# The last step of a recurrent scan in two halves of positions, with the end rows reordered in time

## The chip, the cores and the metric

One core of one Trainium2 chip runs the whole kernel. The metric is device time in microseconds (us). TensorE is PE in the profile (its weight loads PEld), VectorE is DVE, ScalarE is ACT, GpSimd is POOL, and SyncE (SP) issues all the DMAs of this kernel.

## The reference

The input is r of 8 x 2048 x 512 (batch, position, channel). A first part adds to it the normalized result of a long convolution with a state-space kernel; it is unchanged here. Call its result x. The second part is a gated recurrence over the batch axis, 8 steps, for each of the 2048 positions:

```python
def step(c, xt):
    ft = jax.nn.sigmoid(xt @ wf.T + c @ uf.T + bf)
    it = jax.nn.sigmoid(xt @ wi.T + c @ ui.T + bi)
    gt = jnp.tanh(xt @ wc.T + c @ uc.T + bc)
    c = ft * c + it * gt
    return (c, None)
c_final, _ = lax.scan(step, c0, x)
h = jnp.tanh(jnp.einsum('tbi,oi->tbo', x, wo) + c_final @ uo.T + bo)
...
x = x + _layernorm(h)
```

Here xt is the layer norm of x at step t. The output h at every step needs c_final of its position, the state after the last step: for any position, nothing of the output can be finished before all 8 steps are done.

## The kernel before

**Tiling.** The 2048 positions are cut into 4 blocks of 512 (`q`), each of four chunks of 128 (`cj`). Blocks follow one another; in each, 8 steps (`t`) follow one another, so there are 32 (block, step) pairs, about 64 us each. A matrix product of 512 x 512 by 512 x 512 is done by a scheme of seven products of 256 x 256 blocks (`FIRST` holds four of them, `THEN` three), each in split half precision with three products, so a gate *unit* is 42 matmuls with x and 42 with the state. A unit makes one gate (`kind` 0 forget, 1 input, 2 candidate) for one of two halves of the gate's rows (`mp`); there are six units in a step, and two *z units* (42 matmuls each) which make x @ wo.T and store it in `z_d`. Each moving operand is 256 columns (`BP`), the positions.

A unit's PSUM tile `u` (name `u`, pool `pu`, three buffers) holds four 256-wide sums. `part_a` (L974) does the matmuls of `FIRST` and then, on ACT (L993) and DVE (L994 to L997), the sums between them; `part_b` (L999) does those of `THEN` and the gate's tanh on ACT (L1021). With kind 2 DVE joins two gates (L1026), with kind 0 it makes the new state (`state`, L1030: L1041, L1042). After a block's last step the state is split into two half-precision tiles `cf` (ACT L1047, DVE L1051).

**Order of the work.** The order on PE, ACT, DVE, POOL and SP is the program's own. `put` hangs functions on numbered places, 16 to a step, and `go(p)` calls those of place p after a unit's part has been issued; so an instruction stands in its engine's queue behind all that was issued before it, and a DMA that waits holds up the DMAs behind it on SP. In a step, part a of one unit is followed by part b of the unit before. Into the steps of block q are woven `turn` (the next step's x, transposed and split), `prep` (the next rows of x) and the *heads* of block q-1 (`head`, L1130): for each of its 32 rows of 128 positions x 512 channels they load z, add the product of the final state on POOL (L1136), take tanh on ACT (L1139), norm statistics on DVE, the scale on POOL, the normalization on ACT (L1153) and the last sum on POOL (L1154), and store. A head starts every 3 places.

**The end.** The last block has no later block to hide in. After its last step, `last` (L1072) makes the four chunks' output sums (c_final @ uo.T), 48 matmuls of 512 columns into two `u` tiles; the 512 x 512 weights `uw` and the bias `bo` were loaded during the step. All four chunks need the state of all positions to be done. `out` (L1102) adds the bias in place (DVE L1104). Then 16 *rows* (`tail`, L1161), each of two steps of one chunk, go through these stages, `n` being the row:

```python
        for n in range(len(rows) + 5):
            if n % 4 == 0 and n < len(rows):
                end[10 + n // 4]()
            for st_, d in ((0, -3), (1, -3), (6, 5), (2, 1), (3, 2), (4, 3), (5, 3)):
                if 0 <= n - d < len(rows) and (st_ > 1 or n - d > (2 if st_ else 8)):
                    rows[n - d][st_]()
```

Stages 0 and 1 load z and x, stage 2 adds the output sum to z on DVE (L1187, one input in PSUM) and takes tanh on ACT (L1188), stage 3 is the norm's statistics on DVE (L462, L464, L465) and the scale on POOL (L471, L475, L476), stage 4 the normalization on ACT (L1195), stage 5 the last sum (L1200, on POOL; of every fourth row one half on DVE), stage 6 the store (L1203). The z and x of the rows lie in tiles that the weights and gates have left.

Of the kernel before, what the change touches and what calls it, by code (L numbers as in the profile page):

```python
# [22 lines left out]
NB = 8  # L23
# [36 lines left out]
def s4_gated_block(ctx, tc, a, dbg=None):  # L60
# [897 lines left out]

    def views(key):
        q, t, kind, n = key  # L960
        xf = xfs[q, t]
        if kind == "z":
# [4 lines left out]
        return ((lambda f, b, l, k: w[:, k, f, int(l), ms], lambda f, b, l, k: xf[:, b, int(l), k]),  # L967
                (lambda f, b, l, k: uw[:, k, f, int(l), ms], lambda f, b, l, k: cf[k][:, b, int(l)]))
# [5 lines left out]
    def part_a(key):  # L974

        q, t, kind, n = key
        z = kind == "z"
        u = units[key] = pu.tile([P, 4, BP], F32, name="u")
        for pr in FIRST:
            mms(u, places(key, pr), *views(key)[0], True, not t or z)  # L980
        if t and not z:
            mms(u, FIRST[0][:1] + FIRST[1] + FIRST[0][1:], *views(key)[1], False, True)
# [4 lines left out]
        else:  # L987
            g = gates[key] = FJ.tile([P, 4, BP], F32, name="gate2", tag="wq") if kind == 2 else FT.tile([P, 4, BP], F32, name=f"gate{kind}")
            c22 = g[:, 2]
        z_, v_ = (UV, UZ) if z else (UZ, UV)  # L990
        u2 = u2p[:, len(u2s) % 2]
# [5 lines left out]
        V.tensor_tensor(u[:, 2:4], u[:, 2:4], u2[:, None].to_broadcast([P, 2, BP]), ALU.add)  # L997

    def part_b(key):  # L999

        q, t, kind, n = key
# [23 lines left out]
        if kind == 2:  # L1025
            V.scalar_tensor_tensor(g, gates.pop((q, t, 1, n)), 1.0, g, ALU.add, ALU.mult)  # L1026
        elif kind == 0:
            return state(q, t, n)

    def state(q, t, n):  # L1030

        f, ig = gates.pop((q, t, 0, n)), gates.pop((q, t, 2, n))
        if t == 0:
            cds[q, n] = FT.tile([P, 4, BP], F32, name=f"cd{n}")
        cd = cds[q, n]
        for h in range(2):
# [6 lines left out]
            if t == NB - 1:  # L1043
                if h == 0:
                    cf = FT.tile([P, 4, 2, BP], F16, name=f"cf{n}", bufs=2 - n)
                    cfs.setdefault((q, t), []).append(cf)
                S.activation(cf[:, hs, 0], cd[:, hs], AF.Copy)  # L1047
# [24 lines left out]
    def last(q):  # L1072
# [3 lines left out]
        def load():  # L1076
            if end:
                u4 = FE.tile([P, KT, 2, H], F16, name="uw", tag="xf")
# [9 lines left out]
        def load_b():  # L1088
            bo = FE.tile([P, H], F32, name="bo", tag="xa", bufs=2) if end else FT.tile([P, H], F32, name="bo", tag="x1r", bufs=2)
            dma(out=bo, in_=a["bo"])  # L1090
            uws.append(bo)

        def sums(cj, ks=(0, 1, 2, 3)):
            cf, i, cs = cfs[q, NB - 1], cj // 2, slice(cj % 2 * P, (cj % 2 + 1) * P)
            if cj not in us:
                us[cj] = us[cj - 1] if end and cj % 2 else pu.tile([P, 4, BP], F32, name="u").rearrange("p (a b) c -> p a (b c)", a=2)
            for k in ks:
                b = ((0, 3), (1, 2))[i][k // 2]
                mm3(us[cj][:, cj % 2], lambda l: cf[k % 2][:, b, l, cs], lambda l: uws[k][:, l], start=(k == 0), stop=(k == 3))

        def out(cj):
            p_ = us[cj][:, cj % 2]  # L1102
            if end:
                V.scalar_tensor_tensor(p_, uws[KT], SW, p_, ALU.mult, ALU.add)  # L1104
                us_[QC * q + cj] = p_
# [14 lines left out]
        if end:  # L1120
            return [load, load_b] + [lambda ks=ks, cj=cj: sums(cj, ks) for ks in ((0, 2), (1, 3)) for cj in range(QC)] + each[1::2]
# [39 lines left out]
    def tail(q, cj, tp, n):  # L1161

        c, s_ = QC * q + cj, {}

        def load():
            w = (3, 1, 5, 2, 6, 0)[n // 3]
            if n % 3 == 0:
                tails[w] = (FW if w < 2 else FV if w == 2 else FT).tile([P, 3, 2, H], F32, name="zz", tag=f"w{w}", bufs=1)
            s_["z"] = tails[w][:, n % 3]
            dma(out=s_["z"], in_=z_d[c, :, 2 * tp : 2 * tp + 2])  # L1170

        def load_x():
            i = (n + 3) % 9
            if n == 15:
                s_["x"] = tails[0][:, 1]
            elif i < 3:
                if i == 0:
                    tails[4] = FT.tile([P, 3, 2, H], F32, name="xw", tag="w4", bufs=1)
# [187 lines left out]
```

## Time and profile before

| What | us |
|---|---|
| median of three runs (2801.1 to 2802.04) | 2801.32 |
| the profiled execution | 2797.84 |
| its span, first to last instruction | 2796.0 |
| PE busy in the span | 2538.4 (91%) |
| DVE, ACT, POOL busy in the span | 2076.8, 1474.4, 1224.0 |
| first matmul of the last step | 2650.64 |
| first of the 48 output sums on PE | 2718.76 |
| DVE's first bias sum (L1104) | 2726.73 |
| issue of the last store | 2792.49 |

The page gives each engine's busy time, then 40 equal slices of the span with the busy share in tenths, then the chain of work that ended last, followed back from the last instruction. In a timeline each line is a start, a length, the engine, the line of code, the operation with its output and inputs, and how many were merged. In a table by windows each engine has its busy time and number of instructions, then come the granted PE clock, the share of the DMA engines and GB/s. Matmuls are pipelined: the distance between two starts is their price, not the length of one.

### The profile page before, as it was taken

To read this page: it belongs to the slowest core of one execution; us is meant where nothing else is said; L and a number is where in the kernel's file an instruction comes from. 1 tells how busy PE (TensorE), PEld (TensorE's weight loads), DVE (VectorE), ACT (ScalarE), POOL (GpSimd) and SP (SyncE) were. 2 spreads that over 40 slices of the span, in tenths; PEclk is the share of its full clock that TensorE was granted. 3 is DMA by queue.
4 is the path that set the end of the run, shared out by engine and by line. 5 is a ranking of instruction groups with operands and counts; after the bars stand their busy time and mean duration, and the time that the engine had idled before them with its cause. 6 is when DMAs were issued, how large, how long until landed. Compare 5 with 4: busy or idle time off the path is not lost.

```text
span 2796.0 us, 59846 instructions
## 1 busy us (share of the span) xinstructions
PE 2538.4 (91%) x23892; PEld 2225.9 (80%) x23892; DVE 2076.8 (74%) x4208; ACT 1474.4 (53%) x3075; POOL 1224.0 (44%) x1520
## 2 busy tenths in 40 slices
PE   4578888896999999999999999999999999999990
PEld 3367777785888888888888887888888788888880
DVE  8878888867667766577887777778777577776748
ACT  8966666654444444445555544455555445544436
POOL 5767777743112211114554531355544124543317
PEclk9799999998999999999999999999999999999995
DMA  6977887887335433235665532355554335543247
GB/s 237 311 232 243 256 257 245 260 282 208 106 75 132 113 90 85 95 91 142 162 178 150 144 103 91 108 165 170 155 165 134 95 94 154 165 124 102 91 168 250
DMA packets 507535, 449.24 MB, mean 161 GB/s; under 512 B 275574, under 2 KB 386680, under 8 KB 502264
## 3 DMA queue, kind: packets, MB, share of 16 engines
q1 hardware_dynamic: 506824, 444.90, 52.9%
q8 instruction: 186, 3.05, 0.4%
q14 instruction: 93, 0.76, 0.1%
q10 hardware_dynamic: 432, 0.52, 0.1%
HBM read 293.58 MB, written 151.78 MB: 159 GB/s over the span
## 4 chain that ended last, share of the span: by engine, by line
PE 63%; DVE 6%; ACT 3%; issue 1%; POOL 1%; DMA 1%; SPq 0%; POOLq 0%; DVEq 0%; ACTq 0%
PE u L955 61%; PE pt L485 2%; DVE u L997 1%; DVE zz L1187 1%; ACT gate L1021 1%; ACT xf L101 0%; PE u L450 0%; DVE sth L462 0%; DVE u2p L994 0%; DVE xf L102 0%; PE u L452 0%; PE u L451 0%; DVE cd L1042 0%; ACT zr L1153 0%; ACT cf L1064 0%
## 5 line engine op out<-in xcount | busy, mean ns | idle before, releaser
L955 PEld LDWEIGHTS <-w 128*128 128x128 f16 x15120 | 1480.8, 98 | 203.2 <-issue 18.9
L955 PE MATMUL u<-xf,w 128*128 128x256 f16 x8064 | 944.1, 273 | 22.9 <-ACT gate L1021 9.6
L955 PE MATMUL u<-cf,w 128*128 128x256 f16 x7056 | 825.6, 273 | 1.2 <-DVE cf L1066 1.2
L1021 ACT ACTIVATE gate<-u,bias 128x512 f32<-128x512 f32 (+1 forms) x384 | 201.0, 574 | 282.4 <-PE u L955 282.1
L993 ACT ACTIVATE u2p<-u 128x256 f32<-128x256 f32 x256 | 96.6, 379 | 425.2 <-PE u L955 425.0
L955 PE MATMUL u<-w,xf 128*128 128x256 f16 x2688 | 310.8, 273 | 3.7 <-DVE u L997 3.7
L1154 POOL TENSOR_TENSOR x1r<-x1r,zr 128x512 f32<-128x512 f32 x96 | 133.5, 1391 | 407.4 <-ACT zr L1153 298.8
L994 DVE TENSOR_TENSOR u2p<-u2p,u 128x256 f32<-128x256 f32 x256 | 106.7, 417 | 275.2 <-ACT u2p L993 273.7
L909 POOL TENSOR_TENSOR xr<-y,xr 128x512 f32<-128x512 f32 x120 | 160.6, 1358 | 304.0 <-ACT y L908 304.0
L955 PEld LDWEIGHTS <-xf 128*128 128x128 f16 x2688 | 263.2, 98 | 36.1 <-DVE u L997 5.2
L997 DVE TENSOR_TENSOR u<-u,u2p 128x512 f32<-128x512 f32 x256 | 179.0, 699 | 8.8
L646 POOL TENSOR_TENSOR u<-xg,u 128x512 f16<-128x512 f32 x104 | 129.1, 1241 | 107.6 <-ACT u L644 106.6
L471 POOL TENSOR_TENSOR rsy<-rsy,nhalf 128x2 f32<-128x2 f32 (+1 forms) x68 | 50.2, 739 | 283.2 <-DVE rsy L465 282.0
L640 POOL TENSOR_TENSOR xg<-xg,mu 128x512 f32<-128x512 f32 x112 | 162.3, 1455 | 6.7 <-DMA xg<-in_xr 6.7
L102 DVE TENSOR_TENSOR x<-pxt,x 128x256 f16<-128x256 f32 x240 | 100.0, 418 | 63.6 <-ACT x L101 62.2
L1026 DVE SCALAR_TENSOR_TENSOR gate<-gate,gate 128x1024 f32<-128x1024 f32 x64 | 90.0, 1406 | 69.5 <-ACT gate L1021 68.3
L1136 POOL TENSOR_TENSOR zr<-zr,ur 128x512 f32<-128x512 f32 x96 | 131.2, 1367 | 21.1 <-DMA zr<-z_d 12.7
L462 DVE BATCH_NORM_STATS2 sty<-y 128x6 f32<-128x512 f32 x120 | 76.9, 681 | 77.1 <-DMA y<-y_d 77.1
L666 PE MATMUL pxt<-x,at 128*128 128x256 f16 x224 | 61.8, 276 | 79.4 <-DVE x L102 78.8
L101 ACT ACTIVATE x<-pxt 128x256 f16<-128x256 f32 x240 | 91.5, 382 | 74.4 <-PE pxt L666 68.7
L451 PE MATMUL pyt<-u,t 128*128 128x128 f16 (+2 forms) x544 | 124.0, 228 | 0.0
L452 PE MATMUL pyt<-u,t 128*128 128x128 f16 (+2 forms) x544 | 123.5, 227 | 0.0
(375 smaller groups left out, 5204.8 us busy)
## 6 DMA issues: line engine op xcount, KB each, us to landing
xs<-in_rr SPq DMA_DIRECT2D x32, 1024.0 KB, 6.0
t<-kpad SPq DMA_DIRECT2D x32, 1024.0 KB, 5.6
y_d<-y SPq DMA_DIRECT2D x30, 1024.0 KB, 7.6
xr<-in_r SPq DMA_DIRECT2D x60, 512.0 KB, 5.5
xa<-x_d SPq DMA_DIRECT2D x120, 256.0 KB, 4.0
y<-y_d SPq DMA_DIRECT2D x59, 512.0 KB, 5.9
x_d<-xr SPq DMA_DIRECT2D x59, 512.0 KB, 3.2
xg<-in_xr SPq DMA_DIRECT2D x28, 1024.0 KB, 8.2
```

Source lines behind the costliest of these rows:

```text
L102: V.tensor_tensor(lo, src, hi, ALU.subtract)
L451: T.matmul(out, lhsT=w(1), rhs=x(0), start=False, stop=False)
L452: T.matmul(out, lhsT=w(0), rhs=x(1), start=False, stop=stop)
L640: Q.tensor_tensor(xg, xg, bc(mu1), ALU.subtract)
L646: (V if g == 2 else Q).tensor_tensor(u[:, js, 1], xg, u[:, js, 0], ALU.subtract)
L909: Q.tensor_tensor(xv, yv, xv, ALU.add)
L955: T.matmul(u[:, d], lhsT=w(f, b, i == 1, k), rhs=x(f, b, i == 2, k), start=opens and bank not in seen, stop=stop and j == len(n) - 1, skip ...
L994: V.tensor_tensor(u2, u2, u[:, UY], ALU.add)
L997: V.tensor_tensor(u[:, 2:4], u[:, 2:4], u2[:, None].to_broadcast([P, 2, BP]), ALU.add)
L1021: act = lambda o, s_, b: S.activation(o, s_, AF.Tanh, scale=gsc[kind], bias=b)
L1136: Q.tensor_tensor(s_["z"], s_["z"], us_[c], ALU.add)
L1154: Q.tensor_tensor(s_["x"], s_["x"], s_["z"], ALU.add)
```

## The change

Three things, all in the last block.

1. In the last step each gate unit is made twice, for positions 0 to 127 and 128 to 255 of the 256 columns (`half`); all six units of the first half, `g`, come before the six of the second, `h`. The z units stay whole. In the 512 positions of the block the first half is chunks 0 and 2, the second chunks 1 and 3. The output sums of chunks 0 and 2 are issued between units of the second half.
2. The end's rows are numbered by chunk in the order 0, 2, 1, 3, and every stage of a row gets a place of its own, written as a time in us from the step's start (`US` turns it into places). Rows 0 to 5 add the output sum on POOL, from a bias sum kept in SBUF; rows 6 to 15 on DVE. One scale on POOL serves two rows (four norms) and now does the addition of epsilon too.
3. The heads of the block before start every 2.5 places instead of every 3, and the tiles that hold z, x, `uw` and `bo` are others.

The core of the diff (loads, tiles and index plumbing left out):

```diff
+    def half(key):
+
+        return slice(key[4] * P, (key[4] + 1) * P) if len(key) > 4 else slice(0, BP)
...
-        u = units[key] = pu.tile([P, 4, BP], F32, name="u")
+        open_(key)
+        fill(key)
+
+    def open_(key):
+
+        t, z = key[1], key[2] == "z"
+        u = units[key] = pu.tile([P, 4, BP], F32, name="u")[:, :, 0 : P if len(key) > 4 else BP]
         for pr in FIRST:
             mms(u, places(key, pr), *views(key)[0], True, not t or z)
+
+    def fill(key):
+
+        q, t, kind, n = key[:4]
+        z, u = kind == "z", units[key]
+        w = u.shape[-1]
         if t and not z:
             mms(u, FIRST[0][:1] + FIRST[1] + FIRST[0][1:], *views(key)[1], False, True)
...
-                V.scalar_tensor_tensor(p_, uws[KT], SW, p_, ALU.mult, ALU.add)
-                us_[QC * q + cj] = p_
+                o = p_ if cj % 2 else FE.tile([P, H], F32, name="ue", tag="xa", bufs=2)
+                V.scalar_tensor_tensor(o, uws[KT], SW, p_, ALU.mult, ALU.add)
+                us_[QC * q + cj] = o
...
+        cj, tp = (0, 2, 1, 3)[r // 4], r % 4
...
+            pair("z", z_d, "rows" if r in (6, 7) else ((7, 3, None, 1, 5, 2)[(r + (r > 7)) // 3], (r + (r > 7)) % 3))
...
+            pair("x", x1_d, ("wl", "y", "ws", "rows", (4, 1), (4, 2), "wl", "y", (2, 2), (6, 0), (6, 1), (6, 2), (0, 0), (0, 1), (0, 2), (4, 0))[r])
 
         def sum_():
+            for z in s_["z"]:
+                (Q if r < 6 else V).tensor_tensor(z, z, us_[c], ALU.add)
+
+        def gate():
+            for z in s_["z"]:
+                S.activation(z, z, AF.Tanh, scale=1.0 / SW)
+
+        def stat():
+            if m == 0:
+                both[0] = [FE.tile([P, 2, *d], F32, name=nm, bufs=2) for nm, d in (("mvb", (2, 2)), ("rsb", (2,)), ("nmb", (2,)))]
+            mv, rs, nm = s_["b"] = both[0]
+            st = FE.tile([P, 2, 6], F32, name="stb", bufs=2)
             for i in range(2):
-                z = s_["z"][:, i]
-                V.tensor_tensor(z, z, us_[c], ALU.add)
-                S.activation(z, z, AF.Tanh, scale=1.0 / SW)
-
-        def stat():
-            s_["s"] = lnscale(lnstat([s_["z"][:, i] for i in range(2)], "h"))
+                V.bn_stats(st[:, i], s_["z"][i])
+            for i in range(2):
+                V.bn_aggr(mv[:, m, i], st[:, i])
+
+        def scale():
+            mv, rs, nm = s_["b"]
+            Q.tensor_scalar(rs, mv[:, :, :, 1], EPS, None, ALU.add)
+            Q.tensor_tensor(rs, rs, nhalf[:, 0:4].rearrange("p (a b) -> p a b", a=2), ALU.pow)
+            Q.tensor_tensor(nm, mv[:, :, :, 0], rs, ALU.mult)
+            Q.tensor_scalar(nm, nm, -1.0, None, ALU.mult)
...
+            for i, (z, x) in enumerate(zip(s_["z"], s_["x"])):
+                (V if i and (r > 13 or r % 4 == 3) else Q).tensor_tensor(x, x, z, ALU.add)
...
     def go(p):
-        for f in todo.pop(p, ()):
-            f()
+        for k in sorted(k for k in todo if k <= p):
+            for f in todo.pop(k):
+                f()
...
-                p = 3 * r + 17 - 16 * t
+                p = (3 * r if q < NQB - 1 else (5 * r + 1) // 2) + 17 - 16 * t
...
+    put((load_uo, load_bo), PL, (2, 4))
+    for p, cj in ((21, 0), (25, 2)):
+        put((lambda cj=cj: end_sums(cj), lambda cj=cj: end_out(cj)), PL, (p, p + 1))
+    for ks, p in (((0, 2), 31), ((1, 3), 31.5)):
+        put([lambda ks=ks, cj=cj: end_sums(cj, ks) for cj in (1, 3)], PL, (p, p))
+    US = 1 / 2.6
+    put([lambda cj=cj: end_out(cj) for cj in (1, 3)], PL, (88 * US, 88.5 * US))
+    for r, p in enumerate((3, 3, 3, 11, 11, 11, 20, 20, 28, 28, 28, 28, 28, 28, 30, 30)):
+        put(rows[r][:1], PL, (p,))
+    for r, p in enumerate((12, 12, 12, 20, 31, 31, 85 * US, 88 * US, 30, 30, 30, 30, 31.2, 31.2, 31.2, 31.2)):
+        put(rows[r][1:2], PL, (p,))
+    began = (60, 62.6, 65.2, 67.8, 70.4, 73, 82.5, 85.5)
+    scaled = (75.6, 77.4, 86.6)
+    outs = (79, 81.6, 84, 88, 94, 96.5)
+    for r, f in enumerate(rows):
+        t0 = began[r] if r < 8 else 89 + 3 * (r - 8)
+        t1 = t0 + (5.5 if r < 6 else 1.4)
+        t2 = scaled[r // 2] if r < 6 else 92 + 6 * (r // 2 - 3)
+        t3 = (77.5, 79, 81, 82.5)[r] if r < 4 else t2 + 2 + 1.5 * (r % 2)
+        t4 = outs[r] if r < 6 else t2 + 6.4 + 2.5 * (r % 2)
+        put(f[2:5], PL, (t0 * US, t1 * US, (t1 + (2.5 if r < 6 else 1.5)) * US))
+        if r % 2:
+            put(f[5:6], PL, (t2 * US,))
+        put(f[6:], PL, (t3 * US, t4 * US, (t4 + 2.6) * US))
...
+        q, t = steps[NL]
+        zs = [(q, t, "z", i) for i in range(2)]
+        g, h = [[(q, t, gt, mp, i) for mp in range(2) for gt in (1, 2, 0)] for i in range(2)]
+        A, B = lambda k: [(part_a, k)], lambda k: [(finish, k)]
+        O, F = lambda k: [(open_, k)], lambda k: [(fill, k)]
+        plan = (A(zs[0]) + B(before) + A(zs[1]) + B(zs[0]) + O(g[0]) + O(g[1]) + F(g[0]) + F(g[1]) + B(zs[1]) + B(g[0])
+                + sum((A(k) + B(k_) for k, k_ in zip(g[2:] + h, (g + h)[1:])), []) + B(h[5]))
+        for p, (f, key) in enumerate(plan):
+            f(key, PL + p) if f is finish else f(key)
+            go(PL + p)
+        go(PL + 1000)
```

Place p of the last step is `PL + p`; the list `plan` has one entry per place 0 to 30, A(k) being part a of unit k and B(k) part b, and the places are called in the order of their numbers. The stages' times only order the instructions of each engine; no instruction waits for a time.

## The prediction

> **What bounds the kernel now.** I read first the page's 40 slices (PE full until the last slice, where its clock falls to 5 tenths), then the chain of work that ended last from 2640 us on, then the table by windows, then the timeline of the end. The windows cut the last step and what follows it:
>
> ```profile
> core 0: us, PE busy (x) PEld busy (x) DVE busy (x) ACT busy (x) POOL busy (x), PEclk, DMA share, GB/s
> 2650.00:2719.00 69.00, 69.00 (x634) 61.75 (x632) 34.83 (x63) 23.57 (x49) 10.11 (x14) 1.00 0.46 155
> 2719.00:2730.00 11.00, 10.28 (x48) 4.48 (x46) 7.21 (x12) 4.09 (x8) 0.00 (x0) 1.00 0.68 258
> 2730.00:2750.00 20.00, 0.00 (x0) 0.00 (x0) 19.54 (x44) 13.79 (x22) 15.15 (x23) 0.58 0.48 154
> 2750.00:2770.00 20.00, 0.00 (x0) 0.00 (x0) 19.50 (x41) 14.30 (x22) 18.00 (x28) 0.50 0.81 276
> 2770.00:2796.00 26.00, 0.00 (x0) 0.00 (x0) 16.70 (x33) 12.48 (x19) 20.74 (x27) 0.50 0.75 283
> ```
>
> Until 2719 PE has no gap and DVE, ACT and POOL are half idle or more. Then PE does 48 output sums and stops, and the 16 end rows run alone on DVE (97% busy) and POOL. The chain agrees: PE to 2726.5, then DVE's row instructions, POOL's last sums, the last store at 2792.5, end at 2796.0. So the step is PE's, the 66 us behind it are DVE's and POOL's, and the two stages hardly overlap. One end row reads so:
>
> ```profile
> 2768.18 1.27 DVE L1187 TENSOR_TENSOR zz<-zz,u 128x512 f32<-128x512 f32 x2
> ...
> 2769.38 1.27 DVE L462 BATCH_NORM_STATS2 sth<-zz 128x6 f32<-128x512 f32 x2
> ...
> 2769.61 2.48 POOL L1200 TENSOR_TENSOR xx<-xx,zz 128x512 f32<-128x512 f32 x2
> ...
> 2770.58 0.29 DVE L464 BATCH_NORM_AGGREGATE mvh<-sth 128x2 f32<-128x6 f32 x2
> 2770.98 1.14 DVE L465 TENSOR_SCALAR rsh<-mvh 128x2 f32<-128x2 f32 x1
> ...
> 2772.03 1.27 DVE L1187 TENSOR_TENSOR zz<-zz,u 128x512 f32<-128x512 f32 x2
> ```
>
> Start to start, DVE needs 1.20 (sum) + 1.20 (statistics) + 0.40 (aggregate) = 2.8 us a row; the rest of the 3.85 is L465, two numbers per partition, 0.17 us when POOL is free and 1.14 here, ending just as POOL's L1200 ends (2772.09). Over the end the 16 L465 took 11.3 us. The same blocking shows in DVE instructions with both inputs in SBUF and never in those with one input in PSUM (min/median/max ns):
>
> ```profile
> L1041 DVE SCALAR_TENSOR_TENSOR gate<-gate,cd x112: 678/684/1758, 745.5 to 2721.0; 128x512 f32<-128x512 f32 x112
> L1187 DVE TENSOR_TENSOR zz<-zz,u x32: 673/676/687, 2727.5 to 2780.1; 128x512 f32<-128x512 f32 x32
> ```
>
> **The change, part by part.** Times count from the last step's first matmul, 2650.64 us. The span's end is 145.4.
>
> *Halved gate units on PE.* Before: 120 matmuls that stay whole (two z units, the end of the previous step) and 6x84 = 504 of the gates, all 256 columns wide. A group of 24 takes 2.62 us to the next, 0.109 each: 624 x 0.109 = 68.1, and the last gate ends at 68.3. After: 120 whole and 1008 of 128 columns, each with its own 128x128 weight load. In this stage no row shows that width; the convolution does:
>
> ```profile
> 501.23 0.22 PE L450 MATMUL pyt<-u,t 128*128 128x128 f16 x1
> 501.28 0.23 PE L451 MATMUL pyt<-u,t 128*128 128x128 f16 x1
> 501.34 0.23 PE L452 MATMUL pyt<-u,t 128*128 128x128 f16 x1
> 501.41 0.22 PE L450 MATMUL pyt<-x,m 128*128 128x120 f16 x1
> 501.46 0.22 PE L451 MATMUL pyt<-x,m 128*128 128x120 f16 x1
> 501.51 0.22 PE L452 MATMUL pyt<-x,m 128*128 128x120 f16 x1
> ```
>
> Six in 0.33 us (the next starts at 501.56): 0.055 each, although a load is shown as 98 to 150 ns; loads overlap. The line through 512 columns (0.215) and 256 (0.109) gives 0.056 at 128. Bounds: 0.053 (the 120-column steps) and 0.098 (the load's shown length, if it bound). I take 0.056, the nearest row: 56.4 us against 55.0, so +1.4.
>
> The Trainium skill (TensorE: Matmul & The Clock Gate, Back-to-back issue gap) speaks against this: streams of weight load and matmul sustain about 81 ns at 128 columns. By that the halves would take 81.6 us, PE would end 25 us later, and the change would bring nothing (about 2803 us). The rows above are such a stream and show 55, so the row decides.
>
> *Output sums 0 and 2 go between the gates:* 24 x 0.215 = 5.2 us on PE. *Buffers:* the u tiles rotate by three; with the two sums tiles in the rotation, units h3 and h5 (fourth and sixth of the second half) reuse the buffer of the unit that ended just before, and wait for ACT's reading of it, 0.2 + 0.6 + 0.1 = 0.9 us each (bounds 0, if the order were otherwise, and 1.7, L955's longest wait for ACT). PE's last gate: 13.1 + 56.4 + 5.2 + 1.8 = 76.5, eight later than before, but only 24 output sums are then left (5.2 us instead of 10.3).
>
> *Halved DVE and ACT work in the step.* Rows of 256 take 0.42, of 512 0.69, so 128 about 0.28: halving costs about 5 us of DVE in the step, which was 34.8 of 69 busy. Between a unit's part a and part b stand a 36-matmul and a 48-matmul piece, 4.7 us; the ACT copy and four DVE sums need about 2.0. Hidden; without that cover each unit would cost up to 2 us.
>
> *Heads every 2.5 slots instead of 3* in the last block: 6.4 instead of 5.3 a step, +1.1 us DVE and +4.2 POOL in 64, where DVE shows 44 to 50 and POOL 11 to 35. Taken at nothing, up to 3.5 us (0.5 in each of 7 steps) if ordering makes PE wait. Their loads pass SP earlier; the ring is 0.3 to 0.6 busy there.
>
> *Rows 0 to 7 under PE.* Sums 0 end at 51.3. out(0) stands on DVE behind unit h2's sums, so 56.6. POOL then adds rows 0 to 5, 12 x 1.27 = 15.2, with out(2) at 69.5 in between: done at 75 to 77. Their tanh and statistics stand in the queues behind the parts of h4, h5 and the state: rows 0, 1 and 2 have statistics by 77.7, row 3 not. From 77.7 DVE does the last state, six two-SBUF-input instructions and the wait for ACT, 3.3 us: 81. The remaining sums end at about 84.5; out(1) comes later than that on DVE, so they cost nothing.
>
> *DVE from 81:* 13 statistics x 1.60 = 20.8; sums of ten rows x 1.20 = 12.0; three outs 2.0 before the last statistics; out(1), out(3) 1.4. Each row's statistics now follow its own tanh directly: sum to tanh's end 1.4 instead of 1.2, +0.15 x 10 = 1.5. L465 is gone (now part of POOL's scale). Seven instructions with two SBUF inputs (sums of rows 6 and 7, three outs) meet POOL's 1.26: bounds 0 and 1.26 each, taken 0.7 = 5. Sum 42.7: last statistics at 123.7.
>
> *POOL:* one scale for four norms: the power took 0.57 for one number, 0.72 for two, so 1.0 for four; with add, two products and gaps 1.75 instead of 2 x 1.25. From row 3's statistics (82.6): 7 x 1.75 + 27 outs x 1.26 + 6 blocked by DVE = 52.3: 134.9. By DVE: 123.7 + 1.75 + six outs queued behind the last scale (rows 12 to 15, 7.6) = 133. Both engines meet within 2 us; ACT needs 2.73 a row, under DVE's 3.0.
>
> *End:* last out to the span's end took 3.5 (2792.5 to 2796.0). So 137 to 138 with all collisions; I allow 2 to 3 less, since not all nine blocked instructions will meet a POOL sum: **135**, span 2785.6, 10.4 us shorter. The profiled execution took 2797.84, 1.84 over its span; the runs' median, 2801.32, lies 3.5 above that. 2801.3 - 10.4 = **2791**.
>
> *DMA:* after unit h3's weights are free (69) come 20 loads and 16 stores of 0.52 MB, 18.9 MB in 66 us: 286 GB/s, against 283 in the last window at 0.75 share. It fits, barely. Row 6's x load waits on SP for row 0's store, and four stores stand behind it; loads queued earlier drain by about 97, row 6's out is due about 105.
>
> **Rivals.**
> 1. *The weight load sets PE's pace* (slower). At 0.098, PE ends at 13.1 + 98.8 + 7 = 118.9; then state 4.2, sums 2.6, out 0.7, eight rows 24, outs 1.4, scale, outs and store 12.8: 164.6, median 2821. It decides from 0.079 us per matmul (end behind PE 45.7 + PE's end > 145.4). Against it: the convolution's 0.055. For it: 84 in a row without the 512-wide pieces mixed in. 7%.
> 2. *Something eats the gain* (no change, 2796 to 2804): the ring at 250 GB/s needs 75.6 us from 69, ending near 145; or late tanh and statistics in ACT's and DVE's queues hold h3 to h5 for 2 us each and the heads cost 3.5. For it: rings and engines all near full. 17%, and 4% for worse than that.
> 3. *POOL and DVE miss each other*, row 3's statistics come ahead of the state: POOL 46.3 from 80, and the store: 130, median 2786. For it: L1200 and L1187 run side by side now. 17%.
> 4. *The overlap does not come about*: the scale of rows 2 and 3 stands ahead of the first out on POOL and waits for the state; this I have counted already.
>
> The forecast (2787 to 2795.6) has 55%. Measurements tell about 0.2% (5.6 us): faster by more, cases forecast and 3, 72%; within, 17%; slower, 11%. Range 2782 to 2802: it takes in the collisions' and stalls' bounds and leaves out rival 1 and a little at each end.
>
> **What will show it.** Right: 128-column L955 matmuls 0.056 apart, last gate near 2727, POOL's row sums before 2728, no TENSOR_SCALAR on DVE in the rows, DVE at 3.0 to 3.3 a row, POOL's last out near 2782. Wrong: gaps of 1 us or more in L955 beyond two; DVE's rows still 3.5 apart; POOL waiting for DMA at row 6's out; PE's start of the last step moved from 2650.6.

## The result and the profile after

The changed kernel takes 2805.41 us (median of 19 runs, 2803.21 to 2807.16), the kernel before, on the same chip, 2800.53 (19 runs, 2798.44 to 2802.74): ratio 1.0017, 95% interval 1.0011 to 1.0023. It is slower by 4.9 us where 10.4 less was forecast, outside the range of 2782 to 2802. The profiled execution took 2805.44 us, its span 2803.7 (before 2797.84 and 2796.0).

The last step now begins at 2662.6 and the span ends 141.1 later; before, these were 2650.64 and 145.4. So the part that the change is about did become shorter, by 4.3 us, and the last step began 12 us later. The table by windows of the kernel after has the same columns as that of before; its first line is the fifth step of the last block (t = 4), its others are the last step and the end:

```profile
core 0: us, PE busy (x) PEld busy (x) DVE busy (x) ACT busy (x) POOL busy (x), PEclk, DMA share, GB/s
2456.10:2530.70 74.60, 68.48 (x606) 59.97 (x604) 51.44 (x103) 35.81 (x71) 36.46 (x49) 0.98 0.45 136
2662.60:2731.00 68.40, 66.54 (x1005) 62.11 (x1004) 38.83 (x83) 22.02 (x59) 9.94 (x8) 1.00 0.31 113
2731.00:2745.00 14.00, 11.88 (x168) 9.78 (x166) 11.75 (x30) 9.13 (x23) 8.59 (x9) 1.00 0.88 324
...
2785.00:2803.70 18.70, 0.00 (x0) 0.00 (x0) 7.56 (x12) 6.97 (x10) 14.10 (x14) 0.50 0.43 172
```

The same step of the kernel before, in the same view:

```profile
2452.80:2518.70 65.90, 65.90 (x606) 59.24 (x605) 51.84 (x102) 33.53 (x67) 29.31 (x38) 1.00 0.43 129
```

Both rows have 606 matmuls. Before, PE is busy for all of the 65.9 us; after, the step takes 74.6, of which PE waits 6.1, and it is busy 2.6 longer at a lower clock. That is 8.7 us lost in a step that the halves do not touch; what does touch it is the third edit, the heads that start every 2.5 places. The steps t = 2 and 3 are 1.0 longer and 1.1 shorter, all others equal within 0.1. Another 3.6 us stand ahead of the whole block; the other kernels below, whose code is the same there, begin this block between 0.5 us earlier and 4.5 us later than before, and the profiled execution of before was 2.7 under its median, so I take this for a difference between executions. The two that remain, +8.7 and -4.3, make +4.4, and the medians differ by 4.9.

The rows at 128 columns, in the timeline of PE after (the last bracket is the idle time before a group and what ended it):

```profile
2715.46 1.50 PE L955 MATMUL u<-xf,w 128*128 128x128 f16 x24
2716.80 1.50 PE L955 MATMUL u<-cf,w 128*128 128x128 f16 x24
...
2720.69 1.50 PE L955 MATMUL u<-xf,w 128*128 128x128 f16 x24 [0.38 <-DVE ue L1128]
...
2734.68 1.50 PE L955 MATMUL u<-xf,w 128*128 128x128 f16 x24 [1.86 <-DVE ue L1128]
```

24 take 1.34 us to the next group's start, 0.0558 each. The two waits are for DVE's bias sums of chunks 0 and 2 (L1128); a third, 1.49 for ACT's copy of a z unit (L1023), stands at 14.1. The last gate ends at 78.9, where 76.5 was predicted.

The end of the timeline after, ACT, DVE and POOL (L1222 is the rows' tanh, L1230 and L1232 their statistics, L1237 a part of the scale, L1244 the normalization, L1248 the last sum):

```profile
2780.52 2.92 ACT L1244 ACTIVATE zz<-zz,nmb,rsb 128x512 f32<-128x512 f32 x4
...
2783.34 1.13 ACT L1222 ACTIVATE zz<-zz 128x512 f32<-128x512 f32 x2
2783.99 1.28 DVE L1230 BATCH_NORM_STATS2 stb<-zz 128x6 f32<-128x512 f32 x2 [1.26 <-ACT zz L1222]
...
2787.98 1.27 DVE L1230 BATCH_NORM_STATS2 stb<-zz 128x6 f32<-128x512 f32 x2
2789.18 0.29 DVE L1232 BATCH_NORM_AGGREGATE mvb<-stb 128x2 f32<-128x6 f32 x2
...
2789.94 1.04 POOL L1237 TENSOR_TENSOR rsb<-rsb,nhalf 128x4 f32<-128x4 f32 x1
...
2791.54 8.26 POOL L1248 TENSOR_TENSOR zz<-zz 128x512 f32<-128x512 f32 x6
```

The statistics of the last row end at 2789.47 (126.9 from the step's start), the scale takes 1.94, and then POOL still has six last sums in a row to do: 8.26 us in which DVE does two. They end at 137.2, and 3.9 later the span.

### The profile page after: what moved, and what is told of

It is laid out like the page before. It is cut to its first block, busy times and chain, and to the rows that moved or that the text cites. A ratio compares the mean times of both kernels' runs of the same rounds, so it can differ in the third digit from the quotient of the medians.

```text
span 2803.7 us, 60851 instructions
## 1 busy us (share of the span) xinstructions
PE 2545.3 (91%) x24396; PEld 2234.7 (80%) x24396; DVE 2079.6 (74%) x4219; ACT 1477.3 (53%) x3103; POOL 1234.0 (44%) x1515
## 4 chain that ended last, share of the span: by engine, by line
PE 59%; DVE 7%; ACT 3%; POOL 3%; issue 2%; DMA 1%; SPq 0%; POOLq 0%; DVEq 0%; ACTq 0%
PE u L955 57%; PE pt L485 2%; ACT gate L1036 1%; DVE u L1012 1%; DVE cd L1059 1%; POOL xr L909 1%; ACT xf L101 1%; DVE gate L1058 1%; DMA x1r<-x_d 0%; DVE u2p L1009 0%; DVE xf L102 0%; POOL zz L1248 0%; DVE cf L1087 0%; POOL xx L1248 0%; DVE sty L462 0%
## 5 line engine op out<-in xcount | busy, mean ns | idle before, releaser
L955 PE MATMUL u<-xf,w 128*128 128x256 f16 (+1 forms) x8316 | 947.6, 270 | 29.2 <-ACT gate L1036 9.6
L955 PE MATMUL u<-cf,w 128*128 128x256 f16 (+1 forms) x7308 | 828.1, 269 | 2.0 <-DVE cf L1087 2.0
L1036 ACT ACTIVATE gate<-u,bias 128x256 f32<-128x256 f32 (+2 forms) x396 | 203.1, 564 | 272.5 <-PE u L955 272.1
L1008 ACT ACTIVATE u2p<-u 128x256 f32<-128x256 f32 (+1 forms) x262 | 97.4, 372 | 420.3 <-PE u L955 416.6
L1009 DVE TENSOR_TENSOR u2p<-u2p,u 128x256 f32<-128x256 f32 (+1 forms) x262 | 107.5, 410 | 261.8 <-ACT u2p L1008 260.2
L1178 POOL TENSOR_TENSOR x1r<-x1r,zr 128x512 f32<-128x512 f32 x96 | 133.3, 1388 | 367.4 <-ACT zr L1177 244.2
L909 POOL TENSOR_TENSOR xr<-y,xr 128x512 f32<-128x512 f32 x120 | 161.2, 1364 | 293.6 <-ACT y L908 292.7
L1012 DVE TENSOR_TENSOR u<-u,u2p 128x512 f32<-128x512 f32 (+1 forms) x262 | 179.9, 687 | 9.0
L1160 POOL TENSOR_TENSOR zr<-zr,ur 128x512 f32<-128x512 f32 x96 | 130.0, 1354 | 36.3 <-DMA zr<-z_d 27.2
L1041 DVE SCALAR_TENSOR_TENSOR gate<-gate,gate 128x1024 f32<-128x1024 f32 (+1 forms) x66 | 89.4, 1354 | 64.7 <-ACT gate L1036 63.6
L452 PE MATMUL pyt<-u,t 128*128 128x128 f16 (+2 forms) x544 | 123.7, 227 | 0.0
```

What stands on the lines that cost most here:

```text
L452: T.matmul(out, lhsT=w(0), rhs=x(1), start=False, stop=stop)
L909: Q.tensor_tensor(xv, yv, xv, ALU.add)
L955: T.matmul(u[:, d], lhsT=w(f, b, i == 1, k), rhs=x(f, b, i == 2, k), start=opens and bank not in seen, stop=stop and j == len(n) - 1, skip ...
L1009: V.tensor_tensor(u2, u2, u[:, UY], ALU.add)
L1036: act = lambda o, s_, b: S.activation(o, s_, AF.Tanh, scale=gsc[kind], bias=b)
L1160: Q.tensor_tensor(s_["z"], s_["z"], us_[c], ALU.add)
```

## The experiments

My theory after the result: the heads at 2.5 places cost the 8.7 us, because the heads' tiles and loads do not let them come that much faster; the halves gain what their own end shows, 4.3, and less than forecast since POOL's sums collide with DVE's. The rivals: the stall comes from other parts of the change (tiles, places), or it would have come anyway. The table has all twelve runs; "t=4" is that step's length, "gate" the end of the last gate and "end" the span's end, both from the last step's first matmul; each ratio is to the kernel before, run beside it. The runs stand on several chips, so the ratios are to be compared, not the medians: beside them the kernel before has 2801.75 (e1 to e4), 2799.08 (e5 to e8), 2799.70 (e9 to e11) and 2798.49 (e12). The three lengths are of one profiled execution each; where the code of a stage is the same they agree within 0.2 (t=4 of e3, e7 and e8, the end of after and e5).

| Run | median us | ratio, 95% interval | t=4 | gate | end |
|---|---|---|---|---|---|
| before | 2800.53 | | 65.9 | 68.3 | 145.4 |
| after | 2805.41 | 1.0017, 1.0011 to 1.0023 | 74.6 | 78.9 | 141.1 |
| e1_pitch3 | 2799.03 | 0.9993, 0.9984 to 1.0001 | 66.0 | 81.5 | 143.7 |
| e2_before_heads25 | 2810.36 | 1.0027, 1.0017 to 1.0036 | 73.8 | 68.3 | 145.6 |
| e3_zr5 | 2798.53 | 0.9987, 0.9978 to 0.9996 | 69.2 | 78.7 | 140.9 |
| e4_dve_sums | 2800.72 | 0.9997, 0.9988 to 1.0006 | 65.9 | 80.7 | 145.4 |
| e5_x1r3 | 2802.15 | 1.0013, 1.0004 to 1.0023 | 73.9 | 78.9 | 141.2 |
| e6_heads_late | 2797.75 | 0.9997, 0.9987 to 1.0006 | 65.9 | 81.0 | 143.2 |
| e7_outs_dve | 2794.59 | 0.9981, 0.9972 to 0.9991 | 69.2 | 78.7 | 136.8 |
| e8_sum_ahead | 2795.21 | 0.9989, 0.9980 to 0.9998 | 69.1 | 78.7 | 138.9 |
| e9_mended | 2790.65 | 0.9969, 0.9957 to 0.9980 | 66.2 | 78.9 | 136.1 |
| e10_no_overlap | 2793.33 | 0.9980, 0.9971 to 0.9990 | 66.0 | 78.9 | 139.2 |
| e11_bias_first | 2789.43 | 0.9966, 0.9953 to 0.9978 | 66.2 | 76.4 | 133.5 |
| e12_sums_late | 2798.49 | 1.0001, 0.9991 to 1.0010 | 66.1 | 71.2 | 143.3 |

### The heads alone, taken out and put in

e1_pitch3, the kernel after with the heads every 3 places again:

```diff
-                p = (3 * r if q < NQB - 1 else (5 * r + 1) // 2) + 17 - 16 * t
+                p = 3 * r + 17 - 16 * t
```

> The changed kernel with one line put back: the heads of the block before start every 3 places in the last block, as in the kernel before. Theory H (the denser heads cost the time): the step t=4 of the last block, 74.6 us in the trace after against 66.0 before, goes back to 66; the last step and the end keep the 141.1 us that the trace after shows from the last step's first matmul (145.4 before). Together about 4 us faster than the kernel before, ratio 0.9985, some 8.6 us faster than the changed kernel. Rival L (the halved step and the end lose by themselves, and the long step t=4 is an accident of one execution): ratio stays at 1.001 to 1.002.

e2_before_heads25, the kernel before with this line of the change and nothing else (the same lines, the other way round).

> The kernel before with one line of the change alone: heads every 2.5 places in the last block. Theory H: a stall of PE of about 8 us in step t=4 of the last block, where POOL also has three groups of the next rows' sums, and nothing gained at the end: 8 us slower than before, ratio 1.003. Rival L: no stall, ratio 1.000. A third way: heads that end earlier leave the last step freer, but PE was full there, so no gain is expected.

Measured: without the fast heads t=4 falls from 74.6 to 66.0; with them alone in the kernel before it rises from 65.9 to 73.8, and the ratio is 1.0027 (median 2810.36 against 2801.75 beside it). One line makes the stall, with or without the halves. But the slow heads are no free cure in the kernel after: the last of them now stand in the last step, PE waits 2.71 there for ACT's copy of a z unit, and the end is at 143.7 instead of 141.1. That is what the 2.5 bought: 2.6 us, for 8.7. So e1's ratio, expected at 0.9985, is 0.9993, which these runs do not tell from 1.

### Why the heads stall: buffers, or density

A head's first instruction is the load of its z tile, L1133 in the kernel before and L1157 after. The waits in SP's queue from 2380 to 2530 (who waited for whom: total us, times, longest): the three largest rows of the kernel before, where L916 is the store of the next rows and L1157 the head's store, and then the largest of the kernel after, where L1157 is the z load:

```profile
SPq L916 <- POOL xr L909: 52.1, 5, 16.0
SPq L1157 <- POOL x1r L1154: 43.4, 6, 17.0
SPq L1133 <- ACT gate L1021: 3.0, 1, 3.0
```

```profile
SPq L1157 <- POOL x1r L1178: 71.1, 11, 14.1
```

Before, the z load hardly waits. After, it waits for the last sum (L1178) of the head four before it, which gives back the z tile that it takes over. There are four z tiles, and a head holds its own for 10 places, from its load to its sum: at 3 places between heads four tiles make 12, at 2.5 exactly 10, with nothing to spare. Summed over all rows, SP waits no longer than before, 102.8 of the 150 us instead of 107.5; what changed is which instruction stands first in the queue. SP is one queue, so whatever loads stand behind the z load wait too (timeline of SP after, then before):

```profile
2453.51 0.42 SPq L1181 DMA_DIRECT2D out<-x1r  x1
2463.88 0.32 SPq L1157 DMA_DIRECT2D zr<-z_d  x1
2464.30 0.38 SPq L916 DMA_DIRECT2D x_d<-xr  x1
2464.72 0.52 SPq L885 DMA_DIRECT2D y<-y_d  x1
```

```profile
2443.79 0.45 SPq L1133 DMA_DIRECT2D zr<-z_d  x1
2457.18 0.32 SPq L916 DMA_DIRECT2D x_d<-xr  x1
2457.55 0.52 SPq L885 DMA_DIRECT2D y<-y_d  x1
```

After, from 2453.9 to 2463.88 SP issues nothing, until the sum that ends at 2463.85; the load of the next rows' y (L885) comes behind, 8.6 us into the step t=4. Before, SP stands still even longer, from 2444.2 to 2457.18, but with the z load already out, and the load of y comes 4.7 us into the step.

PE waits five times in this step of the kernel after. The longest, 2.72, goes through a z load (timeline of the kernel after, all engines, cut):

```profile
2482.45 1.26 POOL L1178 TENSOR_TENSOR x1r<-x1r,zr 128x512 f32<-128x512 f32 x1
2483.74 0.32 SPq L1157 DMA_DIRECT2D zr<-z_d  x1
...
2487.45 0.39 SPq L1173 DMA_DIRECT2D x1r<-x_d  x1
...
2491.26 1.26 POOL L1178 TENSOR_TENSOR x1r<-x1r,zr 128x512 f32<-128x512 f32 x1 [3.23 <-issue]
...
2494.68 0.23 POOL L476 TENSOR_SCALAR nmx<-nmx 128x2 f32<-128x2 f32 x1
2494.94 1.52 ACT L941 ACTIVATE xa<-xa,nmx,rsx 128x512 f32<-128x512 f32 x2 [5.97 <-POOL nmx L476]
2495.81 1.82 PE L485 MATMUL pt<-cst,xa 128*128 128x128 f32 x8 [2.72 <-ACT xa L941]
```

The z load waits until POOL's sum ends, at about 2483.7, and the next head's load of x (L1173) leaves SP behind it at 2487.45. Such a load took about 3.4 us to land here, and POOL begins that head's last sum at 2491.26. The scale of the next step's x (L476) stands behind it in POOL's queue, ACT's normalization of that x (L941) waits for the scale, and PE's transposes (L485) wait for ACT.

The wait of 1.33 before it has another start. Its chain of waits, in order of time (start, length, engine, tile, line):

```profile
2445.84 5.32 DMA x1r<-x_d
2451.32 1.31 POOL x1r L1178
...
2461.64 2.21 POOL x1r L1178
2463.85 1.24 POOL zr L1160
2465.11 0.63 ACT zr L1163
2465.74 0.98 ACT gate L1036 x2
...
2472.00 1.27 DVE cf L1087 x3
```

A load of x lands late. SP came to it late after a wait of 5.7 for the single tile of the chunk's product (L1155) and a store that took 4.39 to issue, not after a wait for a z tile. POOL's sums (L1178) come late, between them the next rows' sums (L909, in the left-out part), and behind them the next head's z sum (L1160); the head's tanh on ACT (L1163) waits for POOL, and the gate's tanh (L1036) stands behind it in ACT's queue. DVE then makes the state late, and PE waits (PE's timeline of the kernel after):

```profile
2472.47 2.23 PE L955 MATMUL u<-cf,w 128*128 128x256 f16 x19 [1.33 <-DVE cf L1087]
```

Three edits tell buffers from density apart. e3_zr5 gives the heads a fifth z tile (all five places that name the pool):

```diff
-            s_["z"] = FT.tile([P, H], F32, name="zr", bufs=4)
+            s_["z"] = FT.tile([P, H], F32, name="zr", bufs=5)
```

> The changed kernel, heads every 2.5 places, with five instead of four buffers for the heads' z rows. Theory Hb (the stall comes from the buffers: a head's z load stands on SP until the head four before it has done its last sum on POOL, which lies 10 places after its own load, exactly four heads at 2.5): the loads go early, ACT's tanh no longer waits for POOL's sum in front of the gates, the stall of 8.6 us goes, ratio 0.9985. Theory Hp (POOL has too much to do there, heads at 2.5 places and three groups of the next rows in one step, whatever the buffers): the stall stays within 2 us of 8.6, ratio 1.001 to 1.002.

e5_x1r3 leaves four z tiles and gives the x tiles a third (all three places that name the pool):

```diff
-            s_["x"] = FT.tile([P, H], F32, name="x1r", bufs=2)
+            s_["x"] = FT.tile([P, H], F32, name="x1r", bufs=3)
```

> The changed kernel, heads every 2.5 places, with three instead of two buffers for the heads' x rows and four for z as it was. With five z buffers the step t=4 of the last block shrank from 74.7 to 69.2 us, 3.3 above 65.9, and SP then waited 16 us for x buffers (its x loads behind the store of the head two before). Theory Z (the z buffers are the loop that stalls, the x buffers only the next one): t=4 stays above 72 us, ratio 1.001 to 1.002. Rival X (either buffer loosens the loop): t=4 at about 69 us, ratio 0.999.

e6_heads_late leaves all tiles and starts the first 17 heads every 3 places, the others every 2.5, so that the fast stretch begins with the 18th, in t=4, as the work on the block's next rows ends:

```diff
-                p = (3 * r if q < NQB - 1 else (5 * r + 1) // 2) + 17 - 16 * t
+                p = (3 * r if q < NQB - 1 or r < 17 else (5 * r + 17) // 2) + 17 - 16 * t
```

> The changed kernel, with the heads every 3 places while the next rows of x are still being added (heads 0 to 16, to the start of step t=4) and every 2.5 places after that; buffers as in the changed kernel. Theory Hq (the denser heads stall PE only together with the three groups of next rows in t=2 and t=3, the last of which runs into t=4): t=4 at 66 us, nothing lost later, the last step and end at 141 to 142 us (the heads end at place 3 of the last step instead of 10): ratio 0.9985, 2796 to 2798. Rival Hz (2.5 places against a lifetime of 10 with four buffers stalls anywhere): 3 us or more appear in t=5 or t=6.

Measured: a fifth z tile brings t=4 to 69.2, 5.4 of the 8.7; a third x tile brings 0.7. So the z tiles are the larger part. With five, the load of y comes 5.6 us into the step (8.6 with four), and PE's wait of 2.72 falls to 0.50; the wait of 1.33, whose chain does not begin with a z tile, falls only to 0.90. With five the large row of L1157 is gone from SP's waits, and a next short thing shows: the load of x (L1173) waits for the store that frees its tile, for which SP waited 1.5 in the kernel after (SP's waits of e3_zr5):

```profile
SPq L1173 <- DMA out<-x1r: 16.2, 9, 4.5
```

With the fast stretch later, t=4 is back at 65.9 with four z tiles. The z loads still wait then (39.1 us in this window, 65.2 in the rest of the block), as they do in t=5 and 6 of the kernel after, and there it costs PE next to nothing (t=5 of e6 1.1, t=5 and 6 of the kernel after 0). I read this so: the wait for the z tile hurts where the next rows' loads and work stand behind it, which lasts into t=4. That is not shown alone: the two also meet in t=2 and 3 of the kernel after, and those steps together lose nothing. The last 3.3 us are not parted between the two x tiles, the single tile of the chunk's product (its load waits 13.4 in the kernel after and 16.8 in e3, and not before) and the next rows' work itself; five z tiles and three x tiles together were not tried. In e6 the last heads again come into the last step (PE waits 2.18 there; end 143.2), so its time is that of before.

### The collisions of POOL and DVE

In the kernel after, POOL adds the output sums of rows 0 to 5 while DVE still makes states. The state's instructions (L1058) in the last step of the kernel after, min/median/max ns:

```profile
L1058 DVE SCALAR_TENSOR_TENSOR gate<-gate,cd x6: 392/422/1489, 2708.9 to 2743.3; 128x256 f32<-128x256 f32 x6
```

e4_dve_sums is e1 with these sums on DVE:

```diff
-                (Q if r < 6 else V).tensor_tensor(z, z, us_[c], ALU.add)
+                V.tensor_tensor(z, z, us_[c], ALU.add)
```

> Heads every 3 places, and the output sums of end rows 0 to 5 on DVE instead of POOL. In the trace after, the state of unit h2 took DVE 6.6 us (2726.08 to 2732.7) beside POOL's row sums, against 2.6 for the state of h5 beside an idle POOL, and the bias sum behind it held up PE 1.9 us. Theory C (these collisions cost more than the sums): state of h2 back to about 2.6 us, PE's last gate 2 us earlier, and 1 to 3 us off the time against the run with heads at 3 alone. Rival Q (DVE's queue is the scarcer one: its twelve sums of 0.7 us stand before the halves' sums that PE waits for, and before the statistics): 1 to 4 us more.

The same line in e4:

```profile
L1058 DVE SCALAR_TENSOR_TENSOR gate<-gate,cd x6: 393/418/426, 2702.9 to 2738.7; 128x256 f32<-128x256 f32 x6
```

The collisions are real: without POOL's sums the six take 0.42 each, and one whole state takes 2.6 us instead of 6.4 (e1). But the end is at 145.4 instead of e1's 143.7: the twelve sums are now ahead of the gates' work in DVE's queue, and PE waits 0.8 and 2.2 in new places. The ratios of e1 and e4 are not apart. So the collisions took time, but taking them away in this manner brings nothing: e4 exchanges them for a longer queue on DVE, and what they alone cost the end stays open.

### What holds the end

The six last sums on POOL, and tanh behind four normalizations on ACT, were the suspects that the timeline of the end gave. e7_outs_dve is e3 with all last sums of rows 12 to 15 on DVE, which has little else left:

```diff
-                (V if i and (r > 13 or r % 4 == 3) else Q).tensor_tensor(x, x, z, ALU.add)
+                (V if r > 11 or i and r % 4 == 3 else Q).tensor_tensor(x, x, z, ALU.add)
```

> The changed kernel with five z buffers, and the last eight sums (rows 12 to 15) all on DVE instead of six of them on POOL. In the trace after, behind the last statistics (2789.5) POOL makes a scale and six sums in 8.3 us, blocked twice by DVE's, while DVE waits 3.7 us. Theory D (the end hangs on POOL's 1.27 us a sum, and DVE at 0.68 has room): the last sum 3 to 4 us earlier, from the last step's first matmul to the end 137 to 138 us instead of 140.9. Rival N (the end hangs on the scale and the four normalizations behind it, 1.9 and 3 us, whoever sums): within 1 us of 140.9.

e8_sum_ahead is e3 with the output sum of the next row ahead of the statistics of this one, from row 9 on:

```diff
-        put(f[2:5], PL, (t0 * US, t1 * US, (t1 + (2.5 if r < 6 else 1.5)) * US))
+        put(f[2:5], PL, ((t0 - 0.3 * (r > 8)) * US, t1 * US, (t1 + (2.5 if r < 6 else 1.5)) * US))
```

> The changed kernel with five z buffers, and in rows 9 to 15 each row's output sum on DVE ahead of the statistics of the row before, as the kernel before has it. In the trace after DVE waits 5.4 us in the end for tanh on ACT, which stands behind four normalizations. Theory W (those waits are on the path): the last statistics 2 to 4 us earlier, 137 to 139 us from the last step's first matmul to the end. Rival P (POOL's scales and sums set the pace, DVE's waits are slack): 140 to 141.5 us.

Measured against e3's end of 140.9: 136.8 (-4.1) and 138.9 (-2.0). In the traces both held the end; the ratios (0.9981 and 0.9989, against 0.9987 for e3) do not tell the three kernels apart. In e8 DVE's last statistics end at 120.7, but the last scale then stands behind three last sums on POOL, so that only 2.0 us arrive.

e9_mended joins five z tiles, e7, e8, and heads every 3 places for 17 heads and then every 2.25:

```diff
+                p = (3 * r if q < NQB - 1 or r < 17 else (9 * r + 48) // 4) + 17 - 16 * t
```

> What the runs so far point to, together: five z buffers, heads every 3 places until the next rows are done (heads 0 to 16) and every 2.25 after that, so that they end before the last step; the last eight sums on DVE (4.1 us off the end alone); row sums ahead of the row before's statistics (2.0 us alone). If the parts add up: no step of the last block over 67 us, 134.8 us from the last step's first matmul to the end against 145.4 in the kernel before, ratio 0.996. Rival (both mends take away the same wait, or the heads at 2.25 stall again): 137 us, or a step of 68 and more; ratio 0.998.

e11_bias_first is e9 with the bias sums of chunks 0 and 2 one place earlier, ahead of the next unit's sums on DVE:

```diff
-        put((lambda cj=cj: end_sums(cj), lambda cj=cj: end_out(cj)), PL, (p, p + 1))
+        put((lambda cj=cj: end_sums(cj), lambda cj=cj: end_out(cj)), PL, (p, p))
```

> The mended kernel with the bias sums of chunks 0 and 2 one place earlier, ahead of the halves' sums that stand before them on DVE. In all runs with the halves PE waits 0.4 and 1.6 to 1.9 us for these two bias sums, and POOL's row sums begin after the first. Theory B: both waits go, the last gate comes 2 us earlier, POOL's sums 4 us earlier; 1 to 3 us off the time. Rival: DVE then waits in order for the output sums before it does the next unit's sums, and PE waits for those: 0 to 3 us more.

e9 has t=4 at 66.2 and the end at 136.1, ratio 0.9969. Its two mends of the end do not add up: 4.8 us off e3's 140.9, where 4.1 and 2.0 alone made 134.8 the expectation. In e11 both waits for L1128 are gone from PE, the last gate ends at 76.4 and the span at 133.5. Against e9 its ratio, 0.9966, is no different that these runs can tell; both beat the kernel before and the changed one. The last two instructions of e11's timeline:

```profile
2777.97 2.93 ACT L1244 ACTIVATE zz<-zz,nmb,rsb 128x512 f32<-128x512 f32 x4 [4.29 <-POOL nmb L1239]
2778.81 2.81 DVE L1248 TENSOR_TENSOR zz<-zz 128x512 f32<-128x512 f32 x4 [2.37 <-ACT zz L1244]
```

Four last sums on DVE, 2.81 us together, now follow ACT's normalizations closely, where POOL took 8.26 for six and DVE did two beside it.

### What the overlap itself is worth

e10_no_overlap gives all row stages of e9 a place 23 us later (every time given in us raised by 23); e12_sums_late is e10 with the output sums 0 and 2 behind the last gate, so that no row can be added beside the gates:

```diff
-    for p, cj in ((21, 0), (25, 2)):
-        put((lambda cj=cj: end_sums(cj), lambda cj=cj: end_out(cj)), PL, (p, p + 1))
+    for p, cj in ((30.5, 0), (30.6, 2)):
+        put((lambda cj=cj: end_sums(cj), lambda cj=cj: end_out(cj)), PL, (p, p))
```

> The same kernel with every stage of the end rows put 23 us later in the order, so that no row's sum, tanh or statistics stands ahead of PE's last gate; the halves, the two early output sums and all instructions stay. Theory O (the halves pay only by the rows that run beside PE): rows 0 to 2 and the sums of rows 0 to 5 come back to the end, 9 to 13 us more than the run with the overlap, so slower than the kernel before by 0 to 3 us; the last gate 1 to 2 us earlier, as POOL no longer blocks the state. Rival S (POOL and DVE are held up by one another so much beside PE that little is won there): under 5 us more.

> e10 still had the two output sums 0 and 2 between the gates, and so POOL's twelve row sums stood beside PE's last gates. Here these two sums follow the last gate's unit, ahead of sums 1 and 3, so that no row can be added before PE's gates are over: the halves of the last step stay, and nothing of the 16 rows but their loads lies beside the gates. The rows' scale, outs and tanh keep e10's order.
> Theory (the overlap is what the halves buy, and its POOL part is worth most): PE's last gate comes 5.2 earlier than in e11 (24 output sums fewer ahead of it), at 71 to 72; PE's end stays at about 82 to 84; POOL's twelve row sums (12 x 1.27 = 15.2) move behind it. The end comes 4 to 9 us later than e10's 139.2: 143 to 148 from the last step's first matmul, and the ratio to the kernel before is 1.000 to 1.002.
> Rival (POOL's sums beside DVE and PE cost about what they save, since a DVE instruction with two inputs in SBUF takes 1.4 instead of 0.42 beside them): the end moves by less than 2 us against e10, 137 to 141, with the last gate at 71, and the ratio stays at 0.998.

e10 did not do what it was built for: POOL's twelve sums are first in its queue whatever their place, and still ran beside the gates, from 58.4 on. Only the early tanh and statistics moved, and the end by 3.1 (136.1 to 139.2). In e12 POOL's twelve sums start at 75.0, the last gate is at 71.2, and the end at 143.3, 4.1 behind e10 and 9.8 behind e11. Its ratio is 1.0001: with the heads and the end mended but without the overlap, the halves bring nothing. So the overlap is where the gain is, as the prediction had it; an order of the stages made for the case without overlap was not tried, e12 keeps e10's.

## Why the prediction was wrong

The forecast for the end was 10.4 us less; it came out 4.3 less, and 8.7 were lost elsewhere: 6.1 and 8.7 too low, 14.8 of the 15.3 us between the two differences of medians. Without the 8.7 the time would have been about 2796.7, an estimate, still 5.7 over the forecast. The measured 2805.4 fell where the prediction had put 4%, worse than no change. The last of its signs of being wrong came: PE's start of the last step moved.

- *Halved gate units on PE*: right. 0.0558 per matmul against 0.056 taken; rival 1 and its 0.098 are out, and so is the figure of 81 ns that the Trainium skill (TensorE: Matmul & The Clock Gate, Back-to-back issue gap) gives for such streams. The convolution's six rows were enough to decide it.
- *Output sums 0 and 2, Buffers*: two waits of 0.9 for ACT were expected in h3 and h5; 0.38 and 1.86 came, for DVE's bias sums, which stood behind unit sums in its queue. e11 shows the cause by removing it. A wait of 1.49 at 14.1 (the z unit's tile, with a shorter half unit behind it) was not foreseen. Together 3.7 instead of 1.8, last gate 78.9 instead of 76.5.
- *Halved DVE and ACT work*: hidden, but for that 1.49; beside these three PE has no wait of 0.3 or more in its 128-column stretch.
- ***Heads every 2.5 slots*: this is the step that failed.** "Taken at nothing, up to 3.5 us (0.5 in each of 7 steps)" was argued from busy shares: 44 to 50 of 64 for DVE, 11 to 35 for POOL. The measured cost is 8.7 in one step (7.9 in e2; e1 takes it away). What had no room was the rotation of z tiles, ten places of life in four tiles, and SP's one queue behind it: a fifth tile takes 5.4 of the 8.7 away, and the cause of the other 3.3 stays open. (The engines were also a little fuller than I read: between the steps' own starts, t = 1 to 6 of before, DVE has 45.6 to 52.1 and POOL 17.2 to 38.2.) The z load's row of before does not show it, 3.0 us in the 150; the places of a head and its number of tiles do, in the code. What before did show is that SP's queue stood still for 107.5 of those 150 us, nearly all of it for other instructions. I wrote that the heads' loads "pass SP earlier; the ring is 0.3 to 0.6 busy there", which is about the transfers and not about the tiles they need. The bound of 3.5, spread evenly over steps, was no bound at all.
- *Rows 0 to 7 under PE*: right. POOL's sums end at 77.0 (75 to 77 predicted), the last state at 82.5 (81).
- *DVE from 81*: the last statistics at 126.9 instead of 123.7; 1.5 of this is the later state. The other 1.7 is what is left of several terms. The one that I had put at nothing is DVE's wait for tanh behind four normalizations, 5.4 us from 2729 on and 1.9 in e8; I had ACT at 2.73 a row "under DVE's 3.0" and so at no cost, but its work comes in fours.
- *POOL, End*: last sum at 137.2 instead of 134.9, the scale 1.94 instead of 1.75. Then "I allow 2 to 3 less, since not all nine blocked instructions will meet a POOL sum" was taken off the sum of 138.4; nothing of it came. Worked out, 3.4 (allowance) + 2.3 + 0.4 (end 3.9 for 3.5) = 6.1. e7 shows that the last sums which I listed as "queued behind the last scale" could have stood on DVE.
- *DMA* fitted: its share is 0.88 from 2731 to 2745 and 1.02 from 2740 to 2750, but no wait of PE, DVE, ACT or POOL from 2729 on is put down to a DMA.
- *Rivals*: "something eats the gain" named the heads at 3.5 and the full engines, but priced the first too low to end on the other side. The forecast needed a rival of its own for the heads' tiles, with that place and price; by the code, the distance from which it can decide is a head's life over the number of tiles, 10 / 4 = 2.5 places (no run tries a distance between 2.5 and 3 there).

## What to carry to other kernels

When a stage is started more often, first divide how long one of its tiles lives by how many tiles there are: that is the shortest distance between starts, whatever the engines' busy shares say, and a queue that serves others too (SP here) passes the wait on. The queue's total wait does not show this (107.5 and 102.8 us here); which instruction stands first in it does. And at the end of a kernel count what each engine still has queued behind the last late value, and give it to the engine that is done.

## What the runs showed of the hardware

- PE's clock can fall behind a gap of little more than 2 us. Behind the gap of 2.72 us in the kernel after, 18 matmuls of 256 columns took 2.97 us (0.165 each instead of 0.109), and the granted clock from 2494 to 2500 is 0.72. Behind gaps of 2.71 (e1) and 2.18 (e6), 24 of 128 columns took 2.12 and 2.32 instead of 1.34, and the granted clock from 2660 to 2680 is 0.91 in both. Behind 1.86 and 1.49 (after) there was no loss, and none behind 2.22 in e4 (eleven output sums of 512 columns behind it, 0.22 each from start to start), so these runs give no sure threshold. The Trainium skill (TensorE: Matmul & The Clock Gate, Part 1) has the clock fall after an idle window of about 3.4 us; in these three cases less was enough. Those three stalls cost PE another 1.6 to 1.8 us each (all slow groups behind them counted).
- A DVE instruction with both inputs in SBUF took 1.4 to 1.5 instead of 0.42 us beside POOL's sums. The Trainium skill (SBUF — State Buffer, Who interferes with whom) states that such an instruction contends with a GpSimd instruction that reads SBUF. In e4 the remedy moved the end 1.7 us later (145.4 against 143.7 in e1), since it lengthens DVE's queue.
